# Two graph attentions: queries and softmax weights move to PSUM, weighted rows to buffers of their own

## The chip, the cores and the metric

The kernel runs on one core of a Trainium2 chip. The metric is the device time of one execution in microseconds (us). It is taken as the median of several runs; a separate execution is recorded by the profiler. The engines are named PE (TensorE), DVE (VectorE), ACT (ScalarE), POOL (GpSimd) and SP (SyncE). SBUF is the on-chip working memory, PSUM the accumulators' memory.

## The reference, cut to what matters

Four pairs of a graph layer and a feed-forward layer work on 3125 nodes with 256 features; the graph has 103125 edges. Two of the graph layers are attentions and are touched here. The second reads, shortened:

```
Q, K, V = (h @ Wq), (h @ Wk), (h @ Wv)            # 8 heads of 32
score = sum_d(Q[dst] * K[src]) / sqrt(32) + edge_term
alpha = softmax of score over the edges of one dst
out   = segment_sum(alpha * V[src], dst) @ Wo + bo
```

The first is the same with 4 heads of 64, with K and V rows that depend on the edge's type as well, no edge term, and an output matrix chosen by the node's type. The edge term of the second, `relu(efeat @ W1 + b1) @ W2 + b2`, does not depend on the nodes.

## The kernel before, in words

The nodes are sorted by their number of edges and cut into 25 tiles of 128 nodes, one node to a partition. `CAPS` gives the edges to a node that a tile provides for, 67 down to 22, 859 in all. `parts()` (L2051) cuts the tile of 67 in two (34 and 33) and yields every other tile whole, so there are 26 parts of 22 to 44 columns.

`attend` (L2299) does the attention of both layers and is called twice, from `gnn1_attend` (L2531, "first stage" below) and `gnn2_ordered` ("second stage"). For every part it goes through the columns in chunks of four. A chunk takes one buffer `kv` of the pool `at_kv`, which has 13: 4 rows of 512 floats for each partition, keys in the first half, values in the second. Then:

- L2321: POOL issues one indirect DMA for each column. It fetches, for 128 nodes, the row of the table that an index column in SBUF names (`row_et` or `row_src`). So 859 such gathers a stage, 256 KB each.
- L2326: DVE multiplies the keys by the node's query `q`, in place; L2330: DVE sums the products by head into `s`.
- After the last chunk of the part, the softmax on `s`, in small steps: L2337 adds mask or edge term, L2339 to L2342 take the maximum off, L2345 (ACT) takes the exponential in place, L2347 sums it.
- L2351: DVE multiplies the values of each chunk by the exponentials in `s`, in place in `kv`; L2361: PE adds the rows up in the PSUM tile `u` by products with the identity matrix. The buffer `kv` comes free when PE has read it.
- L2366, L2367: ACT and DVE move `u` to `agg`; then it is divided by the sum and goes through `post`: `turned_tile` (L2398, L2400) transposes it, PE multiplies it by the output matrix, DVE adds it to `x` (L833 in the first stage, L2650 in the second).

So a part's buffers are all held until its softmax is done. 34 to 36 columns are 9 chunks, 44 are 11.

In the first stage, `edge_scores` works out the edge term of the second layer beside the attention, one step for each chunk: PE products `ph` (L258), ReLU `eh` on ACT (L1972), PE products `psc` (L1979), `sc` on ACT (L1984), transposes `pst` on PE (L1989), `by_edge` on ACT (L1994). Its `psc` and `pst` have one buffer each. The pool for `post` has one buffer for `tt` and one for `o` in the first stage, two of each in the second.

Each engine goes through its own list of instructions in order. The order of these lists is made when the program is built: instructions are placed by priority and by estimated times, and a buffer that has been given away makes the next user wait for the last reader. The lists are fixed afterwards, whatever the real times are. DVE may so have multiplications of the next part ahead of a late step of the softmax of the present one.

Of the kernel before, what the change touches and what calls it, by code (L numbers as in the profile page):

```python
# [23 lines left out]
F = mybir.dt.float32  # L24
I32 = mybir.dt.int32
U32 = mybir.dt.uint32
AF = mybir.ActivationFunctionType
OP = mybir.AluOpType
AX = mybir.AxisListType
BF = mybir.dt.bfloat16  # L30
PSUM = bass.MemoryType.PSUM
DRAM = bass.MemoryType.DRAM

P = 128
# [6 lines left out]
D = 256  # L41
# [12 lines left out]
CH = 4  # L54
# [12 lines left out]
class Net:  # L67
# [1862 lines left out]
    def edge_scores(self, ctx):  # L1930
# [20 lines left out]
        def steps():  # L1951
            for e0 in range(0, EP, STEP):
                pairs = min(STEP, EP - e0) // 1024
                runs = 2 * pairs
                ef = wp.tile([P, 2, 512], F, name="ef")
                for k in range(runs):
                    s, i = k % 2, k // 2
                    nc.sync.dma_start(
                        ef[s * 64 : (s + 1) * 64, i, :],
                        a["edge_t"][:, e0 + k * 512 : e0 + (k + 1) * 512],  # L1960
                    )
                hs = []
                for i in range(pairs):
                    h = wp.tile([P, 2, 2, 512], F, name="eh")
                    for f in range(2):
                        ps = ps_h.tile([P, 2, 512], F, name="ph")
                        for s in range(2):
                            half = slice(s * 64, (s + 1) * 64)
                            self.mm(
                                ps[:, s, :], [(w1[half, f * P : (f + 1) * P], ef[half, i, :])]  # L1970
                            )
                        nc.scalar.activation(h[:, f], ps, AF.Relu, bias=b1[:, f, :])  # L1972
                    hs.append(h)
                    yield
                ps = ps_s.tile([P, 512], F, name="psc")
                rows = 32 * runs
                for f in range(2):
                    for k in range(runs):
                        nc.tensor.matmul(  # L1979
                            ps[32 * k : 32 * (k + 1)], w2[:, f, :], hs[k // 2][:, f, k % 2, :],  # L1980
                            start=f == 0, stop=f == 1,
                        )
                sc = wp.tile([P, 512], F, name="sc")
                nc.scalar.activation(sc[:rows], ps[:rows], AF.Identity, bias=b2[:rows])  # L1984
                yield

                ps = ps_s.tile([P, 4, P], F, name="pst")
                for c in range(4):
                    nc.tensor.transpose(  # L1989
                        ps[:, c, :rows], sc[:rows].rearrange("h (p c) -> h c p", c=4)[:, c, :],  # L1990
                        self.ident[:rows, :rows],
                    )
                by_edge = wp.tile([P, 4, 4, heads], F, name="by_edge")
                nc.scalar.copy(  # L1994
                    by_edge[:, :runs].rearrange("p k c h -> p c k h"),
                    ps[:, :, :rows].rearrange("p c (k r) -> p c k r", r=32)[:, :, :, :heads],
                )
                nc.scalar.dma_start(
                    self.score_d[e0 : e0 + runs * 512].rearrange(
                        "(k p c) h -> p k (c h)", c=4, p=P  # L2000
                    ),
                    by_edge[:, :runs].rearrange("p k c h -> p k (c h)"),
                )
                yield
# [294 lines left out]
    def attend(self, heads, q_d, table, rows, extra, post, beside=iter(())):  # L2299
# [3 lines left out]
        nc, tc = self.nc, self.tc  # L2303
        hd = D // heads
        with ExitStack() as sub:
            kvp = sub.enter_context(tc.tile_pool(name="at_kv", bufs=13))
            wp = sub.enter_context(tc.tile_pool(name="at_w", bufs=2))
            psu = sub.enter_context(tc.tile_pool(name="at_u", bufs=2, space=PSUM))
            held = None
            for t, k0, k, first, final in self.parts():  # L2310
                if first:
                    q = wp.tile([P, D], F, name="q")
                    nc.sync.dma_start(q, q_d[t * P : (t + 1) * P])
                s = wp.tile([P, heads, KMAX], F, name="s")
                chunks = []
                for c0 in range(0, k, CH):
                    n = min(CH, k - c0)
                    kv = kvp.tile([P, CH, 2 * D], F, name="kv")
                    for c in range(n):
                        at = OFFS[t] + k0 + c0 + c  # L2320
                        nc.gpsimd.indirect_dma_start(  # L2321
                            out=kv[:, c, :], out_offset=None, in_=table,
                            in_offset=bass.IndirectOffsetOnAxis(ap=rows[:, at : at + 1], axis=0),
                        )
                    next(beside, None)
                    nc.vector.tensor_tensor(  # L2326
                        kv[:, :n, :D], kv[:, :n, :D], q.unsqueeze(1).to_broadcast([P, n, D]),
                        op=OP.mult,
                    )
                    nc.vector.tensor_reduce(  # L2330
                        s[:, :, c0 : c0 + n].rearrange("p h c -> p c h"),
                        kv[:, :n, :D].rearrange("p c (h d) -> p c h d", h=heads),
                        axis=AX.X, op=OP.add,
                    )
                    chunks.append((c0, n, kv))
# [6 lines left out]
                nc.vector.tensor_tensor(  # L2342
                    sk, sk, most.unsqueeze(2).to_broadcast([P, heads, k]), op=OP.subtract
                )
                nc.scalar.activation(sk, sk, AF.Exp)  # L2345
                den = wp.tile([P, heads], F, name="den")
                nc.vector.tensor_reduce(den, sk, axis=AX.X, op=OP.add)  # L2347
                u = psu.tile([P, 2, D], F, name="u")
                for c0, n, kv in chunks:
                    v = kv[:, :n, D:].rearrange("p c (h d) -> p c h d", h=heads)  # L2350
                    nc.vector.tensor_tensor(  # L2351
                        v, v,
                        s[:, :, c0 : c0 + n].rearrange("p h c -> p c h").unsqueeze(3).to_broadcast(
                            [P, n, heads, hd]
                        ),
                        op=OP.mult,
                    )
                    if n % 2:
                        nc.vector.memset(kv[:, n, D:], 0.0)
                    for c in range(0, n, 2):  # L2360
                        nc.tensor.matmul(  # L2361
                            u, self.ident, kv[:, c : c + 2, D:],
                            start=c0 == 0 and c == 0, stop=c0 + c + 2 >= k,
                        )
                agg = wp.tile([P, D], F, name="agg")
# [27 lines left out]

    def turned_tile(self, psum, wp, rows):

        ps = psum.tile([P, 2, P], F, name="tt")
        for c in range(2):
            self.nc.tensor.transpose(ps[:, c, :], rows[:, c * P : (c + 1) * P], self.ident)  # L2398
        sb = wp.tile([P, 2, P], F, name="tt_sb")
# [185 lines left out]
    def gnn2_ordered(self):  # L2585
        nc, tc, a = self.nc, self.tc, self.a
        heads, hd = 8, 32
        with ExitStack() as ctx:
# [44 lines left out]
            with ExitStack() as sub:  # L2633
# [9 lines left out]

                def post(t, agg):
                    at = self.turned_tile(psum, wp, agg)
                    po = psum.tile([P, D], F, name="o")
                    self.mm(
                        po, [(self.ones, bo)] + [(at[:, c, :], wo[:, c, :]) for c in range(2)]
                    )
# [263 lines left out]
```

## Time and profile before

| | us |
|---|---|
| median of 3 runs (7748.85 to 7783.94) | 7778.85 |
| the profiled execution | 7774.44 |
| its span | 7772.7 |
| first stage, first gather to end of the last (2346.52 to 3744.97) | 1398.5 |
| second stage (4467.13 to 5775.95) | 1308.8 |

The profiled execution is 0.06% below the median. The mean granted TensorE clock was 0.787. Over the span PE is busy 62%, DVE 41%, ACT 17%, POOL 46%.

A group's line gives the source line, engine, operation, output and inputs, count; then total busy time and the mean in ns; then the idle time of the engine just before these instructions and what ended most of it. "Issue" means that the profile shows nothing that the engine waited for. A line of the timeline gives start, duration, engine, line, operation, and in brackets the idle time before.

### The profile page before, as it was taken

What the parts mean: (1) busy time and instruction counts of PE and PEld (TensorE: products, weight loads), DVE (VectorE), ACT (ScalarE), POOL (GpSimd) and SP (SyncE); (2) the same over time, 40 slices, a digit from 0 to 9 for tenths busy, and PEclk for the clock granted to TensorE, in tenths of its full rate; (3) what the DMA queues carried; (4) which work ended last, traced back from release to release, by engine and by line L of the source; (5) the groups of instructions that cost most, each with busy time, mean ns of one, the idle gap of its engine ahead of it and who ended that gap; (6) DMA issues with size and microseconds to landing.
All of it is one profiled execution on the core that took longest, in us unless ns stands there. A gap on an engine that the chain in (4) does not pass through costs nothing. (4 is left out here: it accounts for less than half of the span.)

```text
span 7772.7 us, 53026 instructions
## 1 busy us (share of the span) xinstructions
PE 4789.8 (62%) x17097; PEld 2917.2 (38%) x17097; DVE 3206.6 (41%) x5563; ACT 1289.0 (17%) x1898; POOL 3566.9 (46%) x4051
## 2 busy tenths in 40 slices
PE   1463313379885778878539423434452995498998
PEld 0352212244441222222338211111122995387554
DVE  7461101034224566666601255666672002496111
ACT  0000000022111222222013100000000221264222
POOL 3878787710006677776322377777752112100001
PEclk9786656689896888988669766666665997698999
DMA  6203542350336566666225255556641443221000
GB/s 246 86 18 123 178 178 69 92 163 9 139 138 185 166 188 199 198 186 175 86 99 181 90 166 170 171 172 178 183 137 72 168 170 107 102 73 38 9 13 22
DMA packets 424876, 999.32 MB, mean 129 GB/s; under 512 B 115151, under 2 KB 219057, under 8 KB 412942
## 3 DMA queue, kind: packets, MB, share of 16 engines
q0 software_dynamic: 206208, 656.36, 27.6%
q1 hardware_dynamic: 164616, 260.15, 10.3%
q10 hardware_dynamic: 53766, 79.32, 2.8%
q8 instruction: 141, 2.31, 0.1%
q14 instruction: 145, 1.19, 0.1%
HBM read 764.22 MB, written 231.45 MB: 128 GB/s over the span
## 5 line engine op out<-in xcount | busy, mean ns | idle before, releaser
L2321 POOL DMA_INDIRECT kv<-o_kv,row_et x859 | 974.9, 1135 | 432.9 <-issue 227.7
L2361 PE MATMUL u<-kv,ident 128*128 128x512 f32 x1740 | 880.9, 652 | 443.9 <-issue 332.7
L2321 POOL DMA_INDIRECT kv<-o_kv,row_src x859 | 1001.3, 1166 | 310.2 <-issue 229.3
L2145 POOL DMA_INDIRECT dense<-pair,place x859 | 907.5, 1056 | 294.5 <-issue 172.7
L2326 DVE TENSOR_TENSOR kv<-kv,q 128x1024 f32<-128x1024 f32 (+2 forms) x450 | 528.5, 1177 | 1022.1 <-DMA kv<-o_kv,row_src 561.6
L258 PE MATMUL g_u<-h_own,dense_rows 128*128 128x256 f32 x1250 | 389.2, 477 | 749.7 <-issue 234.9
L2361 PEld LDWEIGHTS u<-kv,ident 128*128 128x128 f32 x1740 | 340.7, 207 | 967.1 <-issue 792.0
L258 PEld LDWEIGHTS g_u<-h_own,dense_rows 128*128 128x128 f32 x1250 | 297.5, 246 | 841.1 <-issue 445.4
L2330 DVE TENSOR_REDUCE s<-kv 128x16 f32<-128x1024 f32 (+4 forms) x450 | 518.3, 1165 | 4.2
L2020 POOL DMA_INDIRECT out_dram<-x,order_i x25 | 24.6, 983 | 1051.5 <-DVE x L833 1006.6
L2351 DVE TENSOR_TENSOR kv<-kv,s 128x1024 f32<-128x1024 f32 (+2 forms) x450 | 496.5, 1169 | 0.0
L258 PE MATMUL c_hp<-c_xt,c_w 128*128 128x256 f32 x1536 | 389.6, 410 | 1.3 <-DVE c_xt L1251 1.3
L2028 POOL DMA_INDIRECT o_kv<-kv_rows,order_i x50 | 48.8, 976 | 716.9 <-ACT kv_rows L2524 483.9
L258 PE MATMUL ph<-ef,w 64*128 64x512 f32 x808 | 322.8, 709 | 88.6 <-issue 50.8
L258 PEld LDWEIGHTS c_hp<-c_xt,c_w 128*128 128x128 f32 x1536 | 371.7, 333 | 14.9 <-DVE c_xt L1251 7.5
L258 PE MATMUL c_o<-c_w,c_h 128*128 128x256 f32 x1536 | 351.9, 379 | 0.0
L2271 DVE TENSOR_TENSOR o_acc<-o_acc,g_u 128x256 f32<-128x256 f32 x125 | 52.3, 420 | 692.2 <-PE g_u L258 314.5
L1972 ACT ACTIVATE eh<-ph,b 128x1024 f32<-128x1024 f32 x202 | 224.9, 1114 | 499.5 <-PE ph L258 340.3
L2763 PE MATMUL u<-hs_all,eT_sb 128*128 128x256 f32 x1250 | 293.7, 382 | 21.9 <-ACT eT_sb L2759 21.9
L258 PEld LDWEIGHTS c_o<-c_w,c_h 128*128 128x128 f32 x1536 | 288.8, 191 | 34.9
L2398 PE MATMUL tt<-ident,agg 128*128 128x128 f32 x100 | 31.3, 412 | 420.8 <-DVE agg L2389 318.6
L833 DVE SCALAR_TENSOR_TENSOR x<-o,router_l,x 128x256 f32<-128x256 f32 x200 | 94.3, 484 | 459.2 <-PE o L258 459.2
(428 smaller groups left out, 7403.9 us busy)
## 6 DMA issues: line engine op xcount, KB each, us to landing
dense_rows<-dense SPq DMA_DIRECT2D x125, 640.0 KB
dense<-zero ACTq DMA_DIRECT2D x20, 3200.0 KB
ef<-in_edge_t_dram SPq DMA_DIRECT2D x202, 128.0 KB
number_d<-number SPq DMA_DIRECT2D x125, 160.0 KB
number<-number_d SPq DMA_DIRECT2D x25, 800.0 KB
c_x<-slot_d SPq DMA_DIRECT2D x64, 256.0 KB
result_d<-c_y SPq DMA_DIRECT2D x64, 256.0 KB
dense<-zero SPq DMA_DIRECT2D x5, 3200.0 KB
```

Source lines behind the costliest of these rows:

```text
L258: self.nc.tensor.matmul(ps, lhsT, rhs, start=i == 0, stop=i == len(pairs) - 1)
L833: self.nc.vector.scalar_tensor_tensor(self.x[:, t, :], y, w, self.x[:, t, :], op0=OP.mult, op1=OP.add)
L1972: nc.scalar.activation(h[:, f], ps, AF.Relu, bias=b1[:, f, :])
L2028: self.nc.gpsimd.indirect_dma_start(out=table, out_offset=bass.IndirectOffsetOnAxis(ap=self.order_i[:, t : t + 1], axis=0), in_=rows, in_o ...
L2145: nc.gpsimd.indirect_dma_start(out=dense[t], out_offset=bass.IndirectOffsetOnAxis(ap=place[:, at : at + 1], axis=0), in_=pair[:, at, :], i ...
L2271: nc.vector.tensor_tensor(acc[:, b, :], acc[:, b, :], ps, op=OP.add)
L2321: nc.gpsimd.indirect_dma_start(out=kv[:, c, :], out_offset=None, in_=table, in_offset=bass.IndirectOffsetOnAxis(ap=rows[:, at : at + 1], a ...
L2326: nc.vector.tensor_tensor(kv[:, :n, :D], kv[:, :n, :D], q.unsqueeze(1).to_broadcast([P, n, D]), op=OP.mult,)
L2330: nc.vector.tensor_reduce(s[:, :, c0 : c0 + n].rearrange("p h c -> p c h"), kv[:, :n, :D].rearrange("p c (h d) -> p c h d", h=heads), axis ...
L2351: nc.vector.tensor_tensor(v, v, s[:, :, c0 : c0 + n].rearrange("p h c -> p c h").unsqueeze(3).to_broadcast([P, n, heads, hd]), op=OP.mult,)
L2361: nc.tensor.matmul(u, self.ident, kv[:, c : c + 2, D:], start=c0 == 0 and c == 0, stop=c0 + c + 2 >= k,)
L2763: nc.tensor.matmul(u, et[:, j * P : (j + 1) * P], hs_all[:, b, :D], start=b == 0, stop=b == NT - 1,)
```

## The change

In `attend`:

- The query tile is copied by ACT from SBUF into a PSUM tile `q_ps` (two buffers), and L2326 reads it from there.
- The exponential is written into a PSUM tile `e` (one buffer) and not in place; the sum and the multiplication of the values read it there.
- The weighted values go to a new SBUF tile `wv` of a pool with 6 buffers. PE reads `wv`. So `kv` comes free after DVE's multiplication, `wv` after PE's products.
- `at_kv` has 11 buffers and not 13; `u` has one and not two.

To make room in PSUM, `pst` shares the one buffer of `psc`, and `tt` shares the buffers of `o`.

```diff
-                ps = ps_s.tile([P, 4, P], F, name="pst")
+                ps = ps_s.tile([P, 512], F, name="psc").rearrange("p (c n) -> p c n", c=4)
...
-            kvp = sub.enter_context(tc.tile_pool(name="at_kv", bufs=13))
+            kvp = sub.enter_context(tc.tile_pool(name="at_kv", bufs=11))
+
+            vp = sub.enter_context(tc.tile_pool(name="at_v", bufs=6))
             wp = sub.enter_context(tc.tile_pool(name="at_w", bufs=2))
-            psu = sub.enter_context(tc.tile_pool(name="at_u", bufs=2, space=PSUM))
+            psu = sub.enter_context(tc.tile_pool(name="at_u", bufs=1, space=PSUM))
...
                     nc.sync.dma_start(q, q_d[t * P : (t + 1) * P])
+                    q_ps = psu.tile([P, D], F, name="q_ps", bufs=2)
+                    nc.scalar.copy(q_ps, q)
...
                     nc.vector.tensor_tensor(
-                        kv[:, :n, :D], kv[:, :n, :D], q.unsqueeze(1).to_broadcast([P, n, D]),
-                        op=OP.mult,
+                        kv[:, :n, :D], kv[:, :n, :D],
+                        q_ps.unsqueeze(1).to_broadcast([P, n, D]), op=OP.mult,
                     )
...
-                nc.scalar.activation(sk, sk, AF.Exp)
+                e = psu.tile([P, 512], F, name="e")[:, : heads * k]
+                e = e.rearrange("p (h c) -> p h c", h=heads)
+                nc.scalar.activation(e, sk, AF.Exp)
                 den = wp.tile([P, heads], F, name="den")
-                nc.vector.tensor_reduce(den, sk, axis=AX.X, op=OP.add)
+                nc.vector.tensor_reduce(den, e, axis=AX.X, op=OP.add)
                 u = psu.tile([P, 2, D], F, name="u")
                 for c0, n, kv in chunks:
                     v = kv[:, :n, D:].rearrange("p c (h d) -> p c h d", h=heads)
+                    wv = vp.tile([P, CH, D], F, name="wv")
                     nc.vector.tensor_tensor(
-                        v, v,
-                        s[:, :, c0 : c0 + n].rearrange("p h c -> p c h").unsqueeze(3).to_broadcast(
+                        wv[:, :n, :].rearrange("p c (h d) -> p c h d", h=heads), v,
+                        e[:, :, c0 : c0 + n].rearrange("p h c -> p c h").unsqueeze(3).to_broadcast(
                             [P, n, heads, hd]
                         ),
                         op=OP.mult,
                     )
                     if n % 2:
-                        nc.vector.memset(kv[:, n, D:], 0.0)
+                        nc.vector.memset(wv[:, n, :], 0.0)
                     for c in range(0, n, 2):
                         nc.tensor.matmul(
-                            u, self.ident, kv[:, c : c + 2, D:],
+                            u, self.ident, wv[:, c : c + 2, :],
                             start=c0 == 0 and c == 0, stop=c0 + c + 2 >= k,
                         )
...
-        ps = psum.tile([P, 2, P], F, name="tt")
+        ps = psum.tile([P, 2, D], F, name="o").rearrange("p a d -> p (a d)")
+        ps = ps[:, :D].rearrange("p (c n) -> p c n", c=2)
...
-                    po = psum.tile([P, D], F, name="o")
+                    po = psum.tile([P, 2, D], F, name="o")[:, 0, :]
```

## The prediction

> **What bounds it now.** The chain of waits of the page, which I read first, begins at about 5889 us: it says nothing on the two attentions, which lie before. As everything behind a stage needs its results, a stage counts by its own length, 1398.5 and 1308.8 us. So I went to the groups, then to one tile's lines, then to the timeline.
>
> ```profile
> L2321 POOL DMA_INDIRECT kv<-o_kv,row_et x859 | 974.9, 1135 | 432.9 <-issue 227.7
> L2321 POOL DMA_INDIRECT kv<-o_kv,row_src x859 | 1001.3, 1166 | 310.2 <-issue 229.3
> L2326 DVE TENSOR_TENSOR kv<-kv,q 128x1024 f32<-128x1024 f32 (+2 forms) x450 | 528.5, 1177 | 1022.1 <-DMA kv<-o_kv,row_src 561.6
> ```
>
> Busy and idle of POOL's gathers add up to each stage (974.9 + 432.9; 1001.3 + 310.2), while DVE, the next busiest in the second, waits for the gathers. POOL sets the pace. But is a gather 1135 ns long? By tile (shortest/median/longest ns):
>
> ```profile
> L2321 POOL DMA_INDIRECT kv<-o_kv,row_et x859: 940/946/5632, 2346.5 to 3744.0; - x172
> L2321 POOL DMA_INDIRECT kv<-o_kv,row_src x859: 942/946/8056, 4467.1 to 5775.0; - x172
> ```
>
> The median is 946: most are short and some much longer. The timeline (start, duration) shows which:
>
> ```profile
> 5003.94 1.23 DVE L2326 TENSOR_TENSOR kv<-kv,q 128x1024 f32<-128x1024 f32 x1 [2.34 <-DMA kv<-o_kv,row_src]
> 5004.09 1.89 POOL L2321 DMA_INDIRECT kv<-o_kv,row_src  x1 [0.30 <-issue]
> ...
> 5059.64 0.41 DVE L2650 TENSOR_TENSOR x<-x,o 128x256 f32<-128x256 f32 x1
> 5059.71 0.95 POOL L2321 DMA_INDIRECT kv<-o_kv,row_src  x1 [0.30 <-DVE kv L2326]
> ```
>
> ```profile
> 3018.61 2.34 DVE L2330 TENSOR_REDUCE s<-kv 128x16 f32<-128x1024 f32 x2
> ...
> 3019.81 0.95 POOL L2321 DMA_INDIRECT kv<-o_kv,row_et  x1 [0.30 <-DVE s L2330]
> ```
>
> A gather that begins while DVE multiplies two SBUF tensors ends 0.8 us after that multiplication (5005.17 to 5005.98). Beside a reduction, or beside L2650, whose second operand is in PSUM, it takes its 0.95. I sorted all 1718 gathers by the DVE instruction running when they begin. Mean length beside L2326: 1.42 and 1.40 us (first, second stage); beside L2351: 1.76 and 2.02; beside L2330: 0.948; beside the operations with one PSUM operand, L833, L2367 and L2650 (42 gathers): at most 0.950. The excess over 0.946 is 163 us in the first stage and 190 in the second, all but 4 us of it beside DVE operations with two SBUF operands.
>
> The rest of POOL's time: 0.30 us lie between any two gathers, so its floor is 859 x (0.946 + 0.304) = 1074 us a stage. Above it stand the excess and the waits for buffers (total, times, longest; first stage, then second):
>
> ```profile
> POOL kv L2321 <- PE u L2361: 145.4, 38, 29.5
> ```
>
> ```profile
> POOL kv L2321 <- PE u L2361: 55.6, 31, 9.7
> ```
>
> Counting only what exceeds 0.30, buffers cost 162 us in the first stage and 49 in the second: 1074 + 163 + 162 = 1399; 1074 + 190 + 49 = 1313, against 1308.8.
>
> **The change, part by part.**
>
> *q and e in PSUM.* Both large multiplications keep one SBUF operand, like L833, L2367 and L2650, so the excess beside them goes. What keeps two is small: L2337, L2342, L2389, 0.3 to 0.7 us, about 26 each a stage. The single gathers beside them in the second stage show 1.14 to 1.17: 78 x 0.2 us x half of them meeting a gather = 8 us stay. Gain: 163 - 8 = 155 and 190 - 8 = 182 us. From the other side: nothing, if the new operand forms hold POOL as the old did.
>
> [...]
>
> *DVE's own time.* A product of 1024 elements with a PSUM operand is not in the trace. At 256 elements SBUF with PSUM takes 410 ns (L2367) and two SBUF operands 421 (L2389): no difference. The dearest PSUM row of that size is L833 with 478; scaled, 1.22 x 478/421 = 1.39 us, or +0.17 for 450 multiplications, 77 us a stage. DVE idles 430 (first) and 571 us (second) just ahead of L2326, which hides that, but for two such steps in a part's release chain: 26 x 0.34 = 9 us a stage. I take 0, the nearest row.
>
> [...]
>
> *ACT.* One copy of 128x256 for each tile, 25 a stage. ACT's 128x256 copies take 0.37 us (L2366): 9 us a stage on an engine that is busy 17%; its q has been loaded a tile ahead. 0; at worst all of it, 9. The exponential costs what it did (0.32 to 0.50).
>
> *Buffers of kv.* A chunk is four gathers: 5.0 us at the floor, 1474 x 4 = 5.9 us now. At present a part's first buffer returns about 21.5 us after its last gather: a part with 11 chunks has 2 spare buffers, 11.8 us, and waited 9.7 in the second stage; one of 10 chunks has 17.7 and waited about 4. What is in that time shows in a 36-column part: last gather out 5008.5, last key product 5009.80, L2337 5012.31, L2339 5013.03; then a key product of the *next* part, in front of the rest on DVE's list, waits for its gathers until 5016.02; L2342 5018.42; a second such until 5021.04; L2347 5022.19; first L2351 done 5023.7. PE has read that chunk at 5027.4.
>
> After: 11 buffers, released 3.7 us earlier, and the next part's products can stand in the chain only as far as there are spare buffers. Resetting those times, with the late gather (0.9 us) gone: 11 chunks, none spare: done at 5016.5, POOL stops at 5008.8, stall 7.7. 10 chunks, one spare: 5020.2 - 5013.8 = 6.4. 9 chunks: 5022.8 - 5018.8 = 4.0. 8 or fewer: none. With 2, 4 and 9 such parts: 15 + 26 + 36 = 77 us against 46 in the second stage (49 without its start): +31. If the list keeps the whole chain (16.9 us) however few the buffers: 34 + 48 + 62 + 11 = 155, +109. Below: 0 stalls, -46.
>
> In the first stage PE's list mixes L2361 with the edge term, and PE runs behind: the part multiplied from 3391.59 on had its first products only at 3404.19, and an earlier chunk multiplied by 3001.4 was released at 3009.83. So DVE's release comes 8 to 17 us earlier, against 10 us lost with two buffers; waits later in a part go too. In return, L2351 may now wait for `wv`: after six chunks DVE stands behind PE, with the next part's key products, the reductions and `post` queued behind. Bounds: -100 (only 60 of the 162 stay) and +109 as above. I take 0.
>
> *Wait for wv, second stage.* PE, alone there, needs 1.7 us a chunk even at its slow pace (36 matmul records at 0.43 to 0.86 us), DVE 1.15; the eleventh chunk is ready for writing at 11.5 us and its buffer free at 9.8: no wait.
>
> *Single buffers for u and e, shared psc/pst and tt/o.* Each follows its predecessor already: the next first product comes some 20 us after L2367 in the second stage; in the first, 3 us at worst (3043.9 against 3046.7), off POOL's path unless PE is late. 0; at worst 26 x 3 = 78 us in the first stage, which I count within the +109.
>
> Sum: first stage -155 + 0; second -182 + 31 = -151. 7774.4 - 306 = **7468 us**. The profiled execution is 4 us under the median, which I leave out.
>
> **Rivals.**
>
> *PE sets the first stage.* From 3000 to 3039 PE is never idle and does about 37 columns' worth, 1.07 us for a column at full clock: 917 us a stage, some 990 at the clock of 0.93 that 3100 to 3300 has. That leaves room under 1240, but PE also waits for ACT and DVE in turn. If the first stage stays at its length, only the second gains: 7774 - 151 = 7623.
>
> *The first stage's stalls fall too.* For: 145 of its 162 us are waits for PE, which no longer holds `kv`. Then -155 - 100, and the second stage with no net loss of buffers, -182: 7337.
>
> *Slower: the lock stays, the buffers are lost.* If a product with one SBUF operand still holds POOL, each chunk stays at 5.9 us, and with 11 buffers and the release after 17.8 us the stalls are 2 x 17.8 + 4 x 11.9 + 9 x 6.0 = 137 against 46: +91 in each stage, 7956. Against it: the 42 gathers beside PSUM operands, though those ran beside operations a third as long. It decides once gathers beside L2326 and L2351 still average over about 1.2 us.
>
> *No change:* about half the relief goes in stalls of both stages at their upper bound plus waits for wv (-337 + 218 + some 100).
>
> **Numbers.** Chances: forecast 0.52, PE sets the first stage 0.20, stalls fall too 0.15, slower 0.07, no change 0.06. 0.5% (39 us) is about what a measurement can tell here. Faster is the first three, 0.87. The range takes those in, with some 30 us for what lies about each, and leaves out the last two: 7310 to 7655.
>
> **What will show it.** Right: the mean of L2321 falls from 1135 and 1166 to about 955; L2326 and L2351 stay at 1.22 us; the waits of L2321 name DVE L2351 in place of PE; the stages last about 1243 and 1158 us; L2351 waits little for PE. Wrong: gathers still long beside L2326; POOL's idle time growing by over 100 us in a stage; a L2351 that waits for PE in the first stage and key products late behind it; longer L2326 or L2351.

## The result, and the profile after

The changed kernel took 7823.45 us in the median of 9 runs (7804.48 to 7845.33), the kernel before 7774.31 beside it: a ratio of 1.0066, with a 95% interval of 1.0046 to 1.0086. It is slower by 49 us, where 306 us less were forecast. The profiled execution took 7823.45 us with a span of 7821.7.

One thing must be known to read these numbers and those below: in the traces of the result, of both kernels, TensorE (PE) now and then delivers its products late, by up to 31 us, which the traces from four of the five chips of the experiments do not show; there the kernel before takes 7540 to 7551 us, and the same changed program has a ratio of 0.988. Both readings are taken apart below.

The page of the changed kernel (busy us, mean ns, idle before):

```profile
L2327 POOL DMA_INDIRECT kv<-o_kv,row_et x859 | 812.7, 946 | 678.7 <-DVE wv L2360 354.2
...
L2327 POOL DMA_INDIRECT kv<-o_kv,row_src x859 | 814.2, 948 | 475.8 <-issue 233.3
L2332 DVE TENSOR_TENSOR kv<-kv,q_ps 128x1024 f32<-128x1024 f32 (+2 forms) x450 | 523.5, 1168 | 757.7 <-DMA kv<-o_kv,row_src 429.6
...
L2360 DVE TENSOR_TENSOR wv<-kv,e 128x1024 f32<-128x1024 f32 (+2 forms) x450 | 505.1, 1164 | 155.2 <-PE u L2370 64.6
```

Set against the three group lines of before, a gather has gone from 1135 and 1166 ns to 946 and 948, the median of before: the long ones are gone. DVE's products last as long as they did (1168 against 1177). But POOL's idle time has grown from 432.9 to 678.7 us in the first stage and from 310.2 to 475.8 in the second. POOL's waits in the second stage (total, times, longest), and then in the first:

```profile
POOL kv L2327 <- DVE wv L2360: 219.1, 25, 24.8
```

```profile
POOL kv L2327 <- DVE wv L2360: 354.2, 60, 31.2
```

The waits name DVE and not PE, as the change intends, and are far longer than the 145.4 and 55.6 us for PE before. Each stage from its own trace, "idle" being what POOL waits beyond 0.30 us between two gathers:

| | first stage | long gathers | idle | second stage | long gathers | idle |
|---|---|---|---|---|---|---|
| before | 1398.4 | 163 | 166 | 1308.8 | 190 | 50 |
| after | 1482.4 | 1.5 | 412 | 1287.3 | 3.3 | 216 |
| difference | +84 | -162 | +246 | -22 | -187 | +166 |

The relief came in full. All of it, and 60 us more, went into waits for buffers.

### The profile page after: what moved, and what is told of

It is laid out like the page before. It is cut to its first block, busy times and chain, and to the rows that moved or that the text cites. A ratio compares the mean times of both kernels' runs of the same rounds, so it can differ in the third digit from the quotient of the medians.

```text
span 7821.7 us, 52280 instructions
## 1 busy us (share of the span) xinstructions
PE 4790.8 (61%) x17097; PEld 2921.2 (37%) x17097; DVE 3198.9 (41%) x5563; ACT 1304.6 (17%) x1948; POOL 3219.8 (41%) x4051
## 5 line engine op out<-in xcount | busy, mean ns | idle before, releaser
L2370 PE MATMUL u<-wv,ident 128*128 128x512 f32 x1740 | 905.3, 667 | 569.1 <-DVE wv L2360 416.2
L2327 POOL DMA_INDIRECT kv<-o_kv,row_et x859 | 812.7, 946 | 678.7 <-DVE wv L2360 354.2
L2327 POOL DMA_INDIRECT kv<-o_kv,row_src x859 | 814.2, 948 | 475.8 <-issue 233.3
L2332 DVE TENSOR_TENSOR kv<-kv,q_ps 128x1024 f32<-128x1024 f32 (+2 forms) x450 | 523.5, 1168 | 757.7 <-DMA kv<-o_kv,row_src 429.6
L2370 PEld LDWEIGHTS u<-wv,ident 128*128 128x128 f32 x1740 | 347.0, 211 | 1104.8 <-issue 992.1
L2360 DVE TENSOR_TENSOR wv<-kv,e 128x1024 f32<-128x1024 f32 (+2 forms) x450 | 505.1, 1164 | 155.2 <-PE u L2370 64.6
L2336 DVE TENSOR_REDUCE s<-kv 128x16 f32<-128x1024 f32 (+4 forms) x450 | 519.4, 1166 | 3.2
L232 PE MATMUL tp<-ident,z 128*128 128x128 f32 x250 | 52.1, 378 | 384.6 <-DVE z L178 178.5
```

Source lines behind the costliest of these rows:

```text
L2327: nc.gpsimd.indirect_dma_start(out=kv[:, c, :], out_offset=None, in_=table, in_offset=bass.IndirectOffsetOnAxis(ap=rows[:, at : at + 1], a ...
L2332: nc.vector.tensor_tensor(kv[:, :n, :D], kv[:, :n, :D], q_ps.unsqueeze(1).to_broadcast([P, n, D]), op=OP.mult,)
L2336: nc.vector.tensor_reduce(s[:, :, c0 : c0 + n].rearrange("p h c -> p c h"), kv[:, :n, :D].rearrange("p c (h d) -> p c h d", h=heads), axis ...
L2360: nc.vector.tensor_tensor(wv[:, :n, :].rearrange("p c (h d) -> p c h d", h=heads), v, e[:, :, c0 : c0 + n].rearrange("p h c -> p c h").uns ...
L2370: nc.tensor.matmul(u, self.ident, wv[:, c : c + 2, :], start=c0 == 0 and c == 0, stop=c0 + c + 2 >= k,)
```

## The experiments

**Theory A.** The buffers are held by the order of DVE's list. Key products of the next part stand in it ahead of the softmax of the present one; they wait for gathers, and with them the weighting that frees the first buffer. **Rival B.** PE holds the first stage, through the single buffers in PSUM and through `wv`. A rival of size goes beside A: the time from the last gather to the first free buffer is fixed, whatever stands in the list.

The expectations of the first four were written against 7774 us for the kernel before; on their chip it takes 7551, so ratios and idle times are what compares.

**The softmax first.** `issue_after` puts what its block issues behind the given instruction on the same engine's list, and waits for nothing.

```diff
+            weighted = None
...
+                    with tc.issue_after(weighted.ins) if weighted else nullcontext():
+                        nc.vector.tensor_tensor(
+                            kv[:, :n, :D], kv[:, :n, :D],
+                            q_ps.unsqueeze(1).to_broadcast([P, n, D]), op=OP.mult,
+                        )
+                        nc.vector.tensor_reduce(
...
-                    nc.vector.tensor_tensor(
+                    weighted = nc.vector.tensor_tensor(
                         wv[:, :n, :].rearrange("p c (h d) -> p c h d", h=heads), v,
```

> The changed kernel with one rule for DVE's list: the key products and their sums of a part stand behind the last weighting of values (L2360) of the part before, so that no step of the softmax waits for gathers of the next part. Theory A (buffers are held by DVE's list): in the second stage the first buffer comes back about 9 us after the last gather (last key product and sum 2.1, softmax about 4.5, first weighting 1.2, two hand-overs), so parts of 9 chunks with two spare buffers (10 us) no longer stall, those of 10 and 11 stall by about 4 and 9; POOL's idle time there falls from 212 us to about 50 and the stage from 1287 to about 1130. In the first stage, by A, idle falls from 408 to about 150 and the stage from 1482 to about 1230; total about 7410. Theory B (the first stage is held by PE, through the single buffers of u, psc and o and through wv): the second stage as above, the first stays within 60 of 1482; total about 7660. If DVE's list is not the cause in either stage: 7800 or more.

Measured: 7162.82 us, ratio 0.9491 (0.9471 to 0.9512). First stage 1120.0 us with 46 us idle, second 1115.1 with 40. Theory A, and more than it expected. Every economy in PSUM is still there, and DVE can still wait for `wv`, so B is out as the cause of the first stage's loss on this chip.

**Two more buffers kv.**

```diff
-            kvp = sub.enter_context(tc.tile_pool(name="at_kv", bufs=11))
-            vp = sub.enter_context(tc.tile_pool(name="at_v", bufs=6))
+            kvp = sub.enter_context(tc.tile_pool(name="at_kv", bufs=13))
+            vp = sub.enter_context(tc.tile_pool(name="at_v", bufs=3))
```

> The changed kernel with 13 buffers kv in place of 11 and 3 buffers wv in place of 6; the rest as changed. Theory A (the number of kv buffers): two more buffers are 10 us of gathers for each of 25 parts; stalls of 5.5 to 9 us in the second stage go, idle 212 to under 60, stage about 1130; in the first stage about 200 of 408 us go, stage about 1280; total about 7460. Theory A2 (DVE's list keeps the lag however many buffers there are, since it takes in as many key products of the next part as there are buffers): second stage within 40 of 1287, total within 60 of 7823. Theory B (PE holds the first stage): the second stage gains, the first gains nothing or loses with 3 wv: 1480 or more, total about 7660.

Measured: 7363.16 us, ratio 0.9752 (0.9731 to 0.9774). Second stage 1141.9 us, idle 66, close to what A expected of it (1130, under 60). First stage 1289.1, idle 216: the same as the changed kernel has on such a chip (1288.5 and 219, below). There the two buffers bought nothing, with 3 `wv` and up to 5 key products of the next part ahead of the softmax.

**Only q and the exponentials in PSUM**, weighted in place, 13 buffers:

```diff
-            kvp = sub.enter_context(tc.tile_pool(name="at_kv", bufs=11))
-            vp = sub.enter_context(tc.tile_pool(name="at_v", bufs=6))
+            kvp = sub.enter_context(tc.tile_pool(name="at_kv", bufs=13))
...
-                    wv = vp.tile([P, CH, D], F, name="wv")
...
-                        wv[:, :n, :].rearrange("p c (h d) -> p c h d", h=heads), v,
+                        v, v,
...
-                            u, self.ident, wv[:, c : c + 2, :],
+                            u, self.ident, kv[:, c : c + 2, D:],
```

> Only one half of the change: q and the exponentials in PSUM, with all that this needs (single u, pst in psc, tt in o), but the values are weighted in place in kv, 13 buffers, and PE frees them. Theory A (the loss is that of buffers): gathers 0.95 us, the stalls about those of before (162 and 49) and some more because the gathers are faster (2 spare buffers last 10 us, not 11.8): +30 in each; stages about 1280 and 1165, total about 7515. Theory B (single buffers in PSUM hold PE in the first stage): first stage 1400 or more, second 1165, total about 7640.

Measured: 7301.29 us, ratio 0.9671 (0.9649 to 0.9692), where A's 7515 of 7774 is 0.967. Gathers 946 and 950 ns, stages 1213.5 and 1151.7.

**Only the economies in PSUM**, on the kernel before:

```diff
-                ps = ps_s.tile([P, 4, P], F, name="pst")
+                ps = ps_s.tile([P, 512], F, name="psc").rearrange("p (c n) -> p c n", c=4)
...
-            psu = sub.enter_context(tc.tile_pool(name="at_u", bufs=2, space=PSUM))
+            psu = sub.enter_context(tc.tile_pool(name="at_u", bufs=1, space=PSUM))
...
-        ps = psum.tile([P, 2, P], F, name="tt")
+        ps = psum.tile([P, 2, D], F, name="o").rearrange("p a d -> p (a d)")
+        ps = ps[:, :D].rearrange("p (c n) -> p c n", c=2)
...
-                    po = psum.tile([P, D], F, name="o")
+                    po = psum.tile([P, 2, D], F, name="o")[:, 0, :]
```

> The kernel before with nothing but the economies in PSUM: u has one buffer, pst shares that of psc, tt those of o; q, the exponentials and the weighting stay in SBUF, 13 buffers kv. Theory A: these cost nothing, within 25 us of 7774. Theory B: the first stage grows by 80 us or more, total 7850 or more; the second stage within 10.

Measured: 7542.72 us, ratio 0.9984 (0.9971 to 0.9998). They cost nothing on a chip without late products.

**The changed kernel as it is, on a chip of the experiments:**

> The changed kernel as it is, beside the kernel before on the chip of these experiments, where the kernel before takes 7551 us and not 7774. Theory A (buffers held by DVE's list): the loss belongs to the program, so the ratio is between 0.995 and 1.015 (7515 to 7665), with POOL idle over 300 us in the first stage and over 150 in the second, at gathers of 0.95 us. Rival (part of the first stage's loss, in which the first parts stall 27 to 44 us, comes from the surroundings of those runs): the first stage is shorter here by 100 us or more against the 1321 of the experiment with the single buffers alone, and the ratio is under 0.985.

Measured: 7456.84 us, ratio 0.9884 (0.9863 to 0.9905). Idle 219 and 160 us. The truth is between the two expectations: the losses by buffers are there, but smaller than in the result, and the change gains 91 us instead of losing 49. The profile of the kernel before on such a chip gives the other side:

> The kernel before as it is, for a profile beside those of the experiments. Expected from the experiment with the single buffers alone: first stage 1321 us, second 1291, POOL idle about 81 and 50 in them, total about 7550.

Measured: 7542.73 us (one run); stages 1311.9 and 1289.6 us, idle 86 and 51. Gathers of the kernel before, of the changed one and of the one with the softmax first, all on chips without late products:

```profile
L2321 POOL DMA_INDIRECT kv<-o_kv,row_src x859 | 981.0, 1142 | 311.3 <-issue 217.8 <-PE u L2361 55.1 <-DMA kv<-o_kv,row_src 19.8
L2321 POOL DMA_INDIRECT kv<-o_kv,row_et x859 | 968.5, 1127 | 352.9 <-issue 213.6 <-PE u L2361 68.8 <-DMA kv<-o_kv,row_et 12.5
```

```profile
L2327 POOL DMA_INDIRECT kv<-o_kv,row_src x859 | 814.6, 948 | 420.5 <-issue 209.5 <-DVE wv L2360 163.9 <-DMA kv<-o_kv,row_src 31.1
L2327 POOL DMA_INDIRECT kv<-o_kv,row_et x859 | 812.3, 946 | 485.3 <-issue 207.0 <-DVE wv L2360 186.1 <-DMA kv<-o_kv,row_et 21.3
```

```profile
L2328 POOL DMA_INDIRECT kv<-o_kv,row_src x859 | 817.4, 952 | 300.4 <-issue 210.9 <-DVE wv L2362 40.7 <-DMA kv<-o_kv,row_src 34.4
L2328 POOL DMA_INDIRECT kv<-o_kv,row_et x859 | 816.6, 951 | 311.9 <-issue 212.8 <-DVE wv L2362 48.5 <-DMA kv<-o_kv,row_et 25.6
```

Busy time falls by 166 and 156 us from the first pair to the second and stays in the third; the waits for buffers rise from 55.1 and 68.8 to 163.9 and 186.1, and fall to 40.7 and 48.5 with the rule on DVE's list. In the second stage that rule is the only difference of weight: the order on POOL's and PE's lists is the same in both traces, and ACT's differs by three swaps of neighbours. In the first stage the steps of the edge term also moved on ACT's and PE's lists, so there the experiment does not separate DVE's list from theirs.

How the list does it shows in one part of 9 chunks of the second stage. DVE in the changed kernel (start, duration, idle before); the part's last gather ended at 4870.71:

```profile
4874.67 0.68 DVE L2332 TENSOR_TENSOR kv<-kv,q_ps 128x512 f32<-128x512 f32 x1
4875.38 0.69 DVE L2336 TENSOR_REDUCE s<-kv 128x16 f32<-128x512 f32 x1
4878.93 1.22 DVE L2332 TENSOR_TENSOR kv<-kv,q_ps 128x1024 f32<-128x1024 f32 x1 [2.86 <-DMA kv<-o_kv,row_src]
4880.07 0.64 DVE L2343 TENSOR_TENSOR s<-s,scores 128x272 f32<-128x272 f32 x1
4880.62 1.21 DVE L2336 TENSOR_REDUCE s<-kv 128x32 f32<-128x1024 f32 x1
4881.75 0.43 DVE L2345 TENSOR_REDUCE most<-s 128x8 f32<-128x272 f32 x1
4883.43 1.22 DVE L2332 TENSOR_TENSOR kv<-kv,q_ps 128x1024 f32<-128x1024 f32 x1 [1.25 <-DMA kv<-o_kv,row_src]
4884.57 0.16 DVE L2347 TENSOR_SCALAR most<-most 128x8 f32<-128x8 f32 x1
...
4887.08 5.73 DVE L2360 TENSOR_TENSOR wv<-kv,e 128x1024 f32<-128x1024 f32 x5
```

POOL in the same stretch:

```profile
4879.76 0.95 POOL L2327 DMA_INDIRECT kv<-o_kv,row_src  x1 [0.30 <-issue]
4888.56 0.94 POOL L2327 DMA_INDIRECT kv<-o_kv,row_src  x1 [7.86 <-DVE wv L2360]
```

The part is summed at 4876.07. Then a key product of the next part waits 2.86 us for its gathers, the softmax does two steps, a second key product waits 1.25, the softmax goes on. POOL has filled both spare buffers at 4880.71 and stands until the first weighting ends. The same part with the softmax first, where the last gather ended at 4646.95:

```profile
4651.28 0.69 DVE L2338 TENSOR_REDUCE s<-kv 128x16 f32<-128x512 f32 x1
4652.00 0.65 DVE L2345 TENSOR_TENSOR s<-s,scores 128x272 f32<-128x272 f32 x1
...
4654.77 9.72 DVE L2362 TENSOR_TENSOR wv<-kv,e 128x1024 f32<-128x1024 f32 x9
```

```profile
4657.57 0.95 POOL L2328 DMA_INDIRECT kv<-o_kv,row_src  x1 [0.30 <-issue]
```

The weighting starts 7.8 us after the last gather, not 16.4, and the ninth gather of the next part, the first that needs a buffer back, waits for nothing. Over all parts of the changed kernel's second stage:

| chunks | spare buffers | key products of the next part ahead | last gather to first free buffer | stall of POOL |
|---|---|---|---|---|
| 11 | 0 | 0 | 9.4 to 9.7 | 9.4 to 9.7 |
| 10 | 1 | 1 | 13.4 to 13.6 | 8.4 to 8.6 |
| 9 | 2 | 2 | 15.6 to 17.9 | 5.6 to 7.9 |
| 8 | 3 | 3 | 20.5 to 22.4 | 5.4 to 7.1 |

A spare buffer gives POOL 5.0 us of gathers and puts one more product ahead, which costs 4. So a stall of 5.4 to 9.7 us stays in every part of 8 chunks or more. With the softmax first the column "ahead" is 0 throughout and the time 8.1 to 10.6 us.

**Only the buffers of their own**, q and exponentials in SBUF:

```diff
-            kvp = sub.enter_context(tc.tile_pool(name="at_kv", bufs=13))
+            kvp = sub.enter_context(tc.tile_pool(name="at_kv", bufs=11))
+            vp = sub.enter_context(tc.tile_pool(name="at_v", bufs=6))
...
+                    wv = vp.tile([P, CH, D], F, name="wv")
...
-                        v, v,
+                        wv[:, :n, :].rearrange("p c (h d) -> p c h d", h=heads), v,
...
-                            u, self.ident, kv[:, c : c + 2, D:],
+                            u, self.ident, wv[:, c : c + 2, :],
```

> Only the other half of the change: weighted rows go to 6 buffers wv, kv has 11 buffers and DVE frees them; q and the exponentials stay in SBUF, u has two buffers, psc, pst, tt and o their own. Both theories: gathers stay at 1.13 to 1.17 us. Theory A (DVE's list puts as many key products of the next part ahead of the softmax as there are spare buffers, so that every part stalls by what lies between the landing of the last spare chunk and the first weighting, some 7 us): POOL idle in the second stage about 200 us against 50, in the first 250 or more against 81; total about 7870. Rival A2 (the time from the last gather to the first free buffer is fixed at about 17 us, as in the kernel before): with 5.9 us of gathers for a spare buffer only parts of 9, 10 and 11 chunks stall, by 5, 11 and 17: 123 in the second stage, +73, and as much in the first; total about 7700.

Measured: 7727.57 us, ratio 1.0247 (1.0203 to 1.0291). Gathers 1104 and 1126 ns, idle 211 and 140 us. By size this is nearer to the fixed time, by pattern it is A: parts of 8 chunks stall too (2.0 to 5.5 us in the second stage), where a fixed time forbids it. A's sizes were too large; that a spare buffer lasts longer with long gathers is a part of it only (two of them 10.1 to 11.2 us in the second stage, against 10.0 in the changed kernel). The two halves multiply: 0.9671 x 1.0247 = 0.991, and the whole change has 0.988.

**The softmax first, in the kernel before** (the diff of the first experiment, with `q` for `q_ps` and in place):

> The kernel before with only the rule on DVE's list (key products of a part behind the last weighting of the part before): 13 buffers kv, all in SBUF, in place. Theory A (two separate causes: long gathers beside two SBUF operands, and buffers held by DVE's list): the gathers stay at 1.14 to 1.17 us; POOL idle falls from 50 to about 15 in the second stage and from 81 to about 50 in the first, where PE's late reading stays; total about 7485, ratio 0.991. Rival (the list alone is what the time hangs on, the long gathers are hidden by it): 7300 or less.

Measured: 7494.52 us, ratio 0.9929 (0.9905 to 0.9954); gathers 1138 and 1146 ns, idle 70 and 8. The long gathers and the list are two causes, and neither hides the other.

**The softmax first, 12 buffers kv and 5 wv:**

```diff
-            kvp = sub.enter_context(tc.tile_pool(name="at_kv", bufs=11))
-            vp = sub.enter_context(tc.tile_pool(name="at_v", bufs=6))
+            kvp = sub.enter_context(tc.tile_pool(name="at_kv", bufs=12))
+            vp = sub.enter_context(tc.tile_pool(name="at_v", bufs=5))
```

> The changed kernel with the rule on DVE's list, and 12 buffers kv and 5 wv in place of 11 and 6. Theory A: the first buffer comes back about 9.5 us after the last gather; parts of 10 chunks have two spare buffers (10 us) and no longer stall by 4, those of 11 have one and stall by 5 and not by 10; 25 us less in each stage than with 11 buffers, total about 7115. Rival B (DVE waits for PE to free wv in the first stage): with 5 wv the first stage is not shorter than 1120, total 7140 to 7200.

Measured: 7120.65 us, ratio 0.9438 (0.9417 to 0.9459); stages 1098.9 and 1089.7, idle 26 and 14, near the floor of 1074. On a chip without late products PE does not hold the first stage above 1099 us.

**Only the query in PSUM** (the in-place version, with the exponentials back in `s`):

```diff
-                nc.scalar.activation(e, sk, AF.Exp)
+                nc.scalar.activation(sk, sk, AF.Exp)
```

> Only the query in PSUM; the exponentials stay in SBUF, values are weighted in place, 13 buffers kv, single u, pst in psc, tt in o. In the profile before, the gathers beside the key products (L2326) were too long by 173 x 0.476 = 82 us in the first stage and 195 x 0.455 = 89 in the second, those beside the weighting (L2351) by 76 and 91. Theory A (each operation with two SBUF operands holds POOL by itself): gathers beside key products 0.95 us, those beside the weighting stay at 1.7 to 2.1; against the experiment with both in PSUM (7301) that gives back 76 + 91, total about 7465. Rival (one of the two kinds carries it all): 7301 if it is the key products, 7540 if it is the weighting.

Measured: 7450.58 us, ratio 0.9875 (0.9856 to 0.9894). Sorted by the DVE operation beside them, gathers beside key products last 0.945 us in both stages (about 1.3 in the kernel before on the same chip), those beside the weighting still about 1.9. One part shows both, a gather beside a key product (L2331) and one beside a weighting (L2356):

```profile
4890.32 1.22 DVE L2331 TENSOR_TENSOR kv<-kv,q_ps 128x1024 f32<-128x1024 f32 x1 [2.24 <-DMA kv<-o_kv,row_src]
4890.46 0.95 POOL L2326 DMA_INDIRECT kv<-o_kv,row_src  x1 [0.30 <-issue]
...
4891.80 9.76 DVE L2356 TENSOR_TENSOR kv<-kv,s 128x1024 f32<-128x1024 f32 x9
...
4898.68 1.97 POOL L2326 DMA_INDIRECT kv<-o_kv,row_src  x1 [0.30 <-issue]
```

Each operation with two SBUF operands holds POOL by itself.

**The softmax first, in place, 13 buffers** (the diffs of the first and the third experiment together):

> Query and exponentials in PSUM, the rule on DVE's list, but no buffers wv: in place, 13 buffers kv, PE frees them. Theory A with a use for wv only where PE is late: second stage as with wv (first buffer back some 13 us after the last gather, parts of 11 chunks stall by 3): about 1090; first stage, where PE reads late, POOL idle about 70 as in the kernel before with the same rule: about 1145; total about 7170. If wv has no use at all: 7120, as with 12 and 5 buffers.

Measured: 7198.72 us, ratio 0.9542 (0.9524 to 0.956); stages 1161.0 and 1083.0, idle 91 and 11. So `wv` is of use in the first stage only; there 67.8 us of POOL's waits end with PE's reading.

**The softmax first, 13 buffers kv and 3 wv** (the diffs of the first and the second):

> The changed kernel with the rule on DVE's list, 13 buffers kv and 3 wv. By the buffers of kv alone: parts of 11 chunks no longer stall; POOL idle 26 and 14 us (with 12 and 5) fall to about 10 and 2; total about 7095. By wv (DVE behind PE in the first stage with only 3): first stage 1130 or more, second 1080, total about 7140.

Measured: 7134.51 us, ratio 0.9455 (0.9437 to 0.9474); stages 1103.4 and 1079.5, idle 31 and 4. Neither expectation whole: the second stage's idle time falls as the first says, the first stage's does not, and in the first stage's last part DVE frees its first buffer 29.6 us after the last gather (15.4 with 12 and 5), and the gap to the second stage grows from 712 to 730 us.

**Late products.** Whether the result's loss belongs to the program was still open, since the changed kernel's trace there and the one with ratio 0.988 hold the same instructions in the same order on every engine throughout the two stages. Both kernels were measured once more:

> The changed kernel as it is, once more. If the pauses of PE belong to the surroundings of single runs: as in the other experiments, ratio 0.986 to 0.991 at a kernel before of about 7550 us; or, if they come back, a kernel before of about 7775 us and a ratio of 1.00 or more. If they belong to neither, the ratio lies between.

> The changed kernel with the rule on DVE's list, 12 buffers kv and 5 wv, once more. At a kernel before of 7550 us: ratio 0.942 to 0.946. At one of 7775 us, by theory A: the first buffer comes back early enough to bear some pauses, ratio under 0.96.

They came to a fifth chip. Measured there: the kernel before 7752.62 us; as changed 7813.07, ratio 1.0097 (1.0061 to 1.0133), idle 392 and 202; the softmax first with 12 and 5 buffers **8178.34 us, ratio 1.0556** (1.05 to 1.0613), stages 1717.8 and 1401.3, idle 646 and 329. Theory A's "under 0.96" is wrong there by far. What PE's readers wait for, first in the 12-and-5 version on a chip without late products, then here:

```profile
ACT agg L2377 <- PE u L2372: 734.6, 52, 23.1
```

```profile
ACT agg L2377 <- remote: 991.5, 25, 62.2
...
DVE wv L2362 <- remote: 354.7, 33, 24.0
```

"Remote" means that no recorded instruction ended when the wait did. All these waits of ACT's copy end with a step of a semaphore that only PE's instructions step, so it is PE's product that comes late and not the reader. Counted from PE's last record to that step, the delays reach 38 us in this trace and 31 us in the result's; in the traces from the other four chips no such wait ends more than 1 us late. The next lines show one case: PE's last product of a part, then the copy that waits for it.

```profile
5211.43 18.61 PE L2372 MATMUL u<-wv,ident 128*128 128x512 f32 x38 [24.03 <-DVE wv L2362]
```

```profile
5261.15 0.37 ACT L2377 COPY agg<-u 128x256 f32<-128x256 f32 x1 [51.50 <-remote]
```

PE is seen until 5230.04; its result is there 31 us later. The granted clock around it (last but two column; PE's busy time is the second number):

```profile
5225.00:5230.00 5.00, 5.00 (x12) 1.90 (x10) 5.00 (x6) 0.00 (x0) 3.78 (x5) 1.00 0.72 210
5230.00:5235.00 5.00, 0.05 (x1) 0.00 (x0) 0.96 (x1) 0.00 (x0) 3.78 (x5) 0.77 0.75 209
5235.00:5240.00 5.00, 0.00 (x0) 0.00 (x0) 0.00 (x0) 0.00 (x0) 3.78 (x5) 0.50 0.69 203
```

The trace of the result shows the same with the changed kernel; PE's products end at 5690.79 there:

```profile
ACT agg L2375 <- remote: 299.2, 10, 48.0
```

```profile
5684.62 6.17 PE L2370 MATMUL u<-wv,ident 128*128 128x512 f32 x14
```

```profile
5721.44 0.37 ACT L2375 COPY agg<-u 128x256 f32<-128x256 f32 x1 [47.98 <-remote]
```

The fall of the clock does not set these pauses apart: it comes mostly 2 to 5 us after PE's last record (after 67 of the 125 pauses of PE over 6 us in the result's trace of the changed kernel), and does so on chips without late products too (after 56 of 93 in the changed kernel's trace there). The first stage's share at a clock of 0.5 goes with the pauses: 41% in the 12-and-5 version there and 11% on a chip without late products. That such a list suffers more (DVE's weightings wait for `wv` behind PE, and all key products of the next part stand behind them) fits the 20 to 49 us from last gather to first free buffer in every part of that first stage, but was not tried. What was tried is whether idle time of PE brings the pauses:

```diff
+                    if heads == 8:
+                        warm = psu.tile([P, D], F, name="warm")
+                        for _ in range(6):
+                            nc.tensor.matmul(
+                                warm, self.ident, kv[:, 0, :D], start=True, stop=True
+                            )
```

> The version with the rule on DVE's list and 12 and 5 buffers, and 6 more products of 128x256 for each chunk of the second stage, into a PSUM tile that nothing reads; each is 0.41 us, 2.5 us for a chunk of 5 us, beside 1.3 us of real products. On a chip without pauses: within 40 us of 7120, since PE is not the bound. On a chip with pauses, if they follow idle times: the second stage, 1401 us there without these products, falls under 1250; if they follow load: it stays or grows, 1400 or more.

> The same version without the added products, on the same chip: about 7120 without pauses (ratio 0.942 to 0.946), about 8180 with them.

Measured: 7134.27 us, ratio 0.9463 (0.9447 to 0.9479), with the added products, 7119.42, ratio 0.9444 (0.9428 to 0.946), without. The chip had no late products. The low clock's share of the second stage fell from 62% to 5%, and the stage took 1088.7 us against 1085.8: a PE at full clock gains nothing on such a chip. Once more:

> As before for this kernel (6 more products of 128x256 for each chunk of the second stage): on a chip without pauses within 40 us of 7134; on one with pauses, if they follow idle times, the second stage falls from 1401 us to under 1250, and if they follow load, it stays or grows.

> The same version without the added products, on the same chip: about 7120 without pauses, about 8180 with them.

Measured: 7135.31 us, ratio 0.9458 (0.9442 to 0.9474), and 7120.93, ratio 0.9441 (0.9425 to 0.9457), again without late products. What makes PE late on some chips stays open.

## Why the prediction was wrong

- **q and e in PSUM: right.** Forecast -155 and -182 us; measured -162 and -187 in the result's traces, (1127 - 946) x 859 = -156 and (1142 - 948) x 859 = -167 on the other chips. Beside the two large products with both operands in SBUF a gather lasts 1.40 to 2.02 us on average in the trace of before, beside those with one in PSUM 0.945 to 0.950 in the changed kernel's. Why two SBUF operands hold it was not shown.
- **DVE's own time: right.** 1168 against 1177 ns.
- **ACT, the single buffers and the wait for wv: right on chips without late products.** The single buffers alone have 0.9984. DVE waits 23.7 us for `wv` behind PE in both stages together; the 1.7 us a chunk of the text are PE's pace at full clock, though, and not at its slow one: in the second stage before, PE's records follow each other every 0.43 us at a clock of 1.0 and every 0.85 at 0.5, so 3.4 us a chunk.
- **Buffers of kv: this step failed.** It said 0 for the first stage and +31 for the second. On chips without late products it is +133 (86 to 219) and +109 (51 to 160), which is nearly the whole gap of 215 us between the forecast gain of 306 us and the measured 91: (133 - 0) + (109 - 31) = 211. The step had seen the right thing, that the next part's products stand in the chain as far as buffers are spare, but took for parts of 9 and 8 chunks stalls of 4.0 and none. Measured are 5.6 to 7.9 and 5.4 to 7.1, since each spare buffer brings its own product into the chain: a part with three spare buffers has three there, where the one part that was read had two. The base was low as well: 7.7 forecast for parts of 11 chunks, 9.4 to 9.7 measured. Most of that is a misread line. The part's last gather is the first of these two, which ends at 5007.23; the text took the end of the second, 5008.49, which is the next part's first:

```profile
5006.29 0.94 POOL L2321 DMA_INDIRECT kv<-o_kv,row_src  x1 [0.30 <-issue]
5007.54 0.95 POOL L2321 DMA_INDIRECT kv<-o_kv,row_src  x1 [0.30 <-issue]
```

Of the 78 us that the second stage missed, the six parts of 8 chunks are 37, and 1.25 us in each of the 15 longer parts is 19. In the sum for the second stage before, 1313 against 1308.8, the waits beyond 0.304 us are 47 and not 49. In the first stage a gain was set against the loss, because PE no longer holds `kv`; the list of the changed kernel puts up to 4 key products ahead there, where that of before has none from the eleventh part on but for one, and the loss won; how it divides among the lists there was not separated.
- **The rest of the result.** The traces of the result have another +113 and +56 us idle (246 - 133, 166 - 109), together with late products. In the second stage the +56 lie in four parts, whose stalls are 19.9, 12.7, 24.5 and 17.3 us against 9.4, 7.2, 1.7 and 0 in the same program without late products; beside each of them ACT's copy of `u` waits for a product that is 15.8, 7.7, 30.6 and 25.4 us late. The fifth chip repeats them: the kernel before loses 3% there, the changed one 5%. That they turn the gain into a loss is shown by the same program on both kinds of chip; why PE is late is not.
- **Rivals.** "PE sets the first stage" is refuted by 1098.9 us for chips without late products; on the others late products do lengthen that stage. "No change", the relief eaten by stalls in both stages, was given 0.06 and is nearest to the mechanism that came: its +109 in each stage are +133 and +109 without late products, +246 and +166 in the result. The sign that the text had named for being wrong, POOL's idle time growing by over 100 us in a stage, is what the profile shows.
- **A better version.** The changed kernel with the softmax first and 12 and 5 buffers has 0.944 of the time of before on two chips, one of them measured twice, and 1.056 on the one with late products. It is better than both kernels only where PE is on time. Of the other versions only the changed kernel was measured on the chip with late products, so none is known to be better everywhere.

## What to carry to other kernels

A buffer comes free when the releasing engine reaches the instruction that frees it: count what stands ahead of that instruction in its list, and what each of those waits for. More buffers need not help while the list lets work of the next part in for each of them: with two more the first stage's idle time was 216 us against 219, though the second's was 66 against 160. Give a relief of one engine its price only after asking whether the buffers behind it return as fast; here a rule on one list was worth 294 us (7457 to 7163), three times the change itself. One program can gain on one chip and lose on another (0.988 and 1.010 here), so measure on more than one.

## What the runs showed of the hardware

In these runs DVE's operations with two SBUF operands held POOL's indirect gathers, each by itself, and those with one operand in PSUM did not: about 1.9 us beside a weighting from SBUF, 0.945 beside a key product with its query in PSUM, in the same run. An operand in PSUM cost DVE's products of 1024 elements nothing (key products 1168 against 1177 ns, weightings 1164 against 1169). On one of five chips, and in the result's runs, PE's results came up to 38 and 31 us after its last recorded product; the same program differed by 5% between such chips, and the version with the softmax first by 15% (7120 and 8178 us).
